# A four-layer macaron kernel on one core: the attention layers put every compute engine in program order, and the last expert's answers leave tile by tile

## The chip, the core and the metric

The kernel runs on one NeuronCore of a Trainium2 chip. The core has TensorE (PE in the profile, with its weight loads as PEld), VectorE (DVE), ScalarE (ACT), GpSimd (POOL) and SyncE (SP, which here only issues DMA transfers). The metric is the device time of one execution, in microseconds.

## The reference

The input x has the shape (4, 512, 128) in float32: four batches of 512 rows. Four layers follow one another, and each is half a feed-forward network, an attention, and half a feed-forward network again, with a layer norm in front of each part and a residual around it:

```
x = x + 0.5 * ffn_l(layernorm(x));  x = x + attn_l(layernorm(x));  x = x + 0.5 * ffn_l(layernorm(x))
```

The parts differ from layer to layer:

- Layer 0: a routed network with 8 experts, the best expert for each row, 320 places per expert, hidden size 512. Its attention has 16 heads of 8, causal, with a table of relative positions added to the scores.
- Layer 1: a gated network with 8 experts (the best two, no limit on places) and a shared one. Its attention scores are a product of two products, `logits = A1 * A2 * SCALE`, with factors of rank 4 and 8 per head, causal.
- Layer 2: a network with 8 experts (the best two), and in place of attention a gated recurrence along the rows.
- Layer 3: a routed network with 8 experts, the best two, 512 places per expert. Its attention has 16 heads of 8 without a mask, and a norm of its own on top of the layer norm.

## The kernel before

x stays in SBUF as `xs[b]`, one tile of 128 x 4 x 128 per batch b: 4 tiles of 128 rows.

**Routed networks** (layers 0 and 3, before and after attention: f00, f01, f30, f31) are the class `Mixture`. `tokens` takes one or two batches: `norms` gives the layer norm (per 128-row tile statistics on DVE at L154 and L155, then `rstd` as a power on POOL at L157, then `off`, then the scaled rows). A transpose, the gate's logits (L310), a softmax (L225 to L232), `route` (L207 to L215) and a rank within the expert (L352 and L353) follow. Then `to` (L373) holds each row's place, and POOL scatters the rows into DRAM with one indirect DMA per 128 rows and choice (`disp_f`, L376). `experts` runs over the 8 experts: it loads the expert's rows (`fetch`), transposes them and works out where each answer goes (`prepare`: `lost`, `back`, L427 to L430), multiplies by the two weight matrices (L445, L461), adds the bias (L465, L469), scales (L472) and scatters the answers to DRAM (`res_f`, L473). `combine` reads the answers back per batch (L484) and adds them to x (L485).

**Attention** is one function for layers 0, 1 and 3. Its work is 16 units, four batches by four groups of four heads. The main loop runs over the units u and in each over four row tiles j. Layers 0 and 1 make scores with a table or mask added (L554, L571, L572, L575, L576) for unit u + 1 while unit u is transposed and copied (`weights`, L587, L594, L596) and multiplied with the values (L607). Layer 3 finds the largest score of each row first (`largest`, L554 and the reductions L629), folds it into q (`lowered`, L635 and L637), makes the scores again by key (`by_key`, L554 and L649), and multiplies with the values (`times_values`, L677). Its `largest` runs `lead = 2*NT + 2` half steps ahead, where a unit has 8. All PSUM tiles come from one ring of 8 banks.

Other work rides in the loop as generators, and a call of `next` moves one of them to its next `yield`, a hop:

- `begin(b)`, by `begun`: norm, transpose, heads and values of the next batch. Layer 1's heads are factors that are copied to SBUF (`fac`, two buffers), written to DRAM in nine transfers per batch (L1086, L1090), and read back per unit by `fetch` (L1106); `project` multiplies them (L1113). In layer 3 `begin` has statistics, `r` as a power on POOL (L1284), `off` (L1285), two scaled copies (L1290, L1295); q and k come from L842, L844 and L846, and per unit `project` makes q and k of a group (L852 on ACT, L1313 on POOL).
- `after(b)`, by `go_on`: `tokens` of f01 or f31 for a batch whose attention has ended.
- `beside`: loads of later weights and zeros for later scatters. For layer 3's feed-forward weights, `moe_weights` puts small POOL copies (L500) ahead of the loads.

The order on each engine comes from two sources. Inside `tc.manual_schedule(engines={mybir.EngineType.PE})` around the loop, PE takes its instructions in the order of the program. The other engines, and all of them outside, are ordered by the tile scheduler from its own cost model, so it can move an instruction ahead of others that the program has first. The hops of the loop are placed so:

```
if j % 2 == 0:
    go_on()
else:
    next(beside, None)
...
if (u % NG, j) in ((0, 1), (1, 1), (1, 3)) and u < n_units - NG:
    begun(u // NG + 1)
if j == 1 and u + 2 < n_units:
    start(u + 2)
if j == 3 and fetch is not None and u + 3 < n_units:
    fetch(*units[u + 3])
```

Of the kernel before, what the change touches and what calls it, by code (L numbers as in the profile page):

```python
# [18 lines left out]
P = 128  # L19
# [23 lines left out]
def kernel(ctx: ExitStack, tc: tile.TileContext, a: dict, out: bass.AP):  # L43
# [102 lines left out]
    def norms(srcs, dsts, tag, scalar=False):  # L146
# [11 lines left out]
        if scalar:  # L158
            off = small.tile([P, g], FP, name=f"off_{tag}", tag=f"bn_off{g}")
            nc.vector.scalar_tensor_tensor(off, mv[:, :, 0], -1.0, rstd, ALU.mult, ALU.mult)  # L160
# [20 lines left out]
    def normed(b, tag, scalar=False):  # L181

        n = work.tile([P, NT, D], FP, name=f"n_{tag}", tag="n", bufs=3)
        norm(xs[b], n, tag, scalar)
        yield
        return n
# [36 lines left out]
    def softmax(pool, lg, g, tag):  # L223
        mx = pool.tile([P, g], FP, name=f"smx_{tag}", tag=f"smx_{tag}")
        nc.vector.tensor_reduce(mx, lg, AX.X, ALU.max)  # L225
        pr = pool.tile([P, g, E], FP, name=f"pr_{tag}", tag=f"pr_{tag}")
        nc.vector.tensor_tensor(pr, lg, bc(mx, [P, g, E]), ALU.subtract)
        nc.scalar.activation(pr, pr, AF.Exp)
        sm = pool.tile([P, g], FP, name=f"sm_{tag}", tag=f"sm_{tag}")
        nc.vector.tensor_reduce(sm, pr, AX.X, ALU.add)  # L230
        nc.vector.reciprocal(sm, sm)
        nc.vector.tensor_tensor(pr, pr, bc(sm, [P, g, E]), ALU.mult)  # L232
        return pr
# [4 lines left out]
    class Mixture:  # L238
# [41 lines left out]
        def tokens(self, bs, wT, scalar=False, pool=None):  # L280
# [8 lines left out]
            for n, b in zip(ns, bs):  # L289
                for c in range(k):  # L290
# [6 lines left out]
                    )  # L297
            yield from norms([xs[b] for b in bs], rows, tag, scalar)
# [22 lines left out]
            pr = softmax(pool, plg[:, : G * E].rearrange("p (g e) -> p g e", e=E), G, f"r{G}")  # L321
# [13 lines left out]
            for i, n in enumerate(ns):  # L335
                for c in range(k):
                    nc.gpsimd.tensor_copy(n[:, :, 1 if c else D + 3], counts[:, c, i * NT : (i + 1) * NT])
# [12 lines left out]
            for c in range(k):  # L350
                out = ps[:, c].rearrange("p g e -> p (g e)")
                nc.tensor.matmul(out, before, masks[:, c].rearrange("p g e -> p (g e)"), start=True, stop=False)  # L352
                nc.tensor.matmul(out, ones, pre[:, c, :G, :].rearrange("p g e -> p (g e)"), start=False, stop=True)  # L353
            kept = tile("kept", [P, k, G, E])
# [3 lines left out]
            if k == 2:  # L358
# [6 lines left out]

            spare = tile("spare", [P, k, G])
            nc.gpsimd.tensor_scalar(
                spare, bc_mid(tok_id[:, i0 : i0 + G], [P, k, G]), float(self.rows), None, ALU.add
            )
# [3 lines left out]
            nc.vector.tensor_tensor(to, slot, keep, ALU.subtract)  # L373
            for c in range(k):
# [9 lines left out]
        def experts(self, w):  # L384
# [3 lines left out]
            with tc.tile_pool(name=f"moe_{self.tag}", bufs=2) as pool:  # L388
# [21 lines left out]
                def prepare(e):  # L410
# [14 lines left out]
                    back = pool.tile([P, per], I32, name=f"back{tag}", tag="back", bufs=3)  # L425
                    lost = pool.tile([P, per], FP, name=f"lost{tag}", tag="lost")
# [9 lines left out]
                for e in range(E):  # L436
# [20 lines left out]
                    y = pool.tile([P, per, D], FP, name=f"y{tag}", tag="y", bufs=3)  # L457
                    for s in range(per):
# [6 lines left out]
                    nc.vector.tensor_tensor(  # L465
                        o[:, :whole, :], po[:, :whole, :], bc_mid(b2[:, e, :], [P, whole, D]), ALU.add
                    )
                    if left:
                        nc.vector.tensor_tensor(o[:left, whole, :], po[:left, whole, :], b2[:left, e, :], ALU.add)  # L469
                    for s in range(per):  # L470
                        m = min(P, cap - s * P)
                        nc.scalar.activation(y[:m, s, :], o[:m, s, :], AF.Copy, scale=d[:m, s, D + 1 : D + 2])  # L472
                        nc.gpsimd.indirect_dma_start(  # L473
                            out=self.back[e * per + s][:, :],
                            out_offset=bass.IndirectOffsetOnAxis(ap=back[:m, s : s + 1], axis=0),
                            in_=y[:m, s, :],
                            in_offset=None,
                        )
# [54 lines left out]
    def attention(pool, tag, begin, project, residual, owT, added, after=None, beside=(), fetch=None):  # L533
# [201 lines left out]
        with tc.manual_schedule(engines={mybir.EngineType.PE}):  # L735
            for _ in range(3):
                begun(0)
# [14 lines left out]
            for u in range(n_units + 1):  # L752
                last = u - 1
                now, nxt = u < n_units, u + 1 < n_units
                for j in range(NT):
# [301 lines left out]
    def l1_attn(first, beside):  # L1057
        with tc.tile_pool(name="attn1", bufs=2) as pool:
# [9 lines left out]
            def begin(b):  # L1068
# [8 lines left out]
                for i, w in enumerate(l1["factors"]):  # L1077
# [7 lines left out]
                    if i == 0:  # L1085
                        nc.sync.dma_start(rows[b][i], f)  # L1086
                        continue
                    for r in range(R1):
                        t = rows[b][i]
# [5 lines left out]
                        )  # L1095
                values(b, nT, l1["wv"], None, f"a1_{b}")
# [169 lines left out]
    def l3_attn(beside, after):  # L1266
        (mixed, bT, wvT, bv), owT, ob, gb = l3["attn"]
        with tc.tile_pool(name="attn3", bufs=2) as pool:
            qk = {}

            def begin(b):
# [12 lines left out]
                nc.gpsimd.tensor_tensor(r, r, mhalf.rearrange("p (k t) -> p k t", k=2), ALU.pow)  # L1284
                nc.vector.scalar_tensor_tensor(  # L1285
# [16 lines left out]
                qk[b] = heads(pool, nT, mixed, bT, tag)  # L1302
                values(b, nT, wvT, bv, tag)
# [136 lines left out]
```

## Time and profile before

| | us |
|---|---|
| median of 3 runs | 1677.62 (1672.47 to 1678.33) |
| the profiled execution, its own time | 1679.45 |
| its span, first to last instruction | 1677.7 |
| PE busy | 1304.1 (78%) |
| DVE busy | 825.1 (49%) |
| ACT busy | 731.5 (44%) |
| POOL busy | 696.3 (42%) |
| mean granted PE clock | 0.872 of full speed |

Stages by the timeline, in us from the start of the span: first tokens and loads 0 to 84, f00's experts 84 to 136, layer 0's attention 137 to 371, f01 to 456, layer 1's first network to 545, its attention 545 to 822, the chain from layer 1's second network to f30's tokens 822 to 1122, f30's experts to 1204, layer 3's attention 1204 to 1541, the last tokens to 1581, f31's experts to 1659, the end at 1677.

How to read it: the profile is one execution. A row of the timeline has the start, the busy time, engine and line, the operation with its tiles and shapes, and in brackets how long the engine was idle before it and what ended that. "PE t_a L587 <- DVE top_a L575" in the view of waits means that PE's next instruction for the tile t_a at line 587 was released by DVE's instruction for top_a. PEclk is the clock that TensorE was granted: at 0.50 a busy PE does half the work. DMA share is the mean busy share of the core's 16 DMA engines.

### The profile page before, as it was taken

To read this page: it belongs to the slowest core of one execution; us is meant where nothing else is said; L and a number is where in the kernel's file an instruction comes from. 1 tells how busy PE (TensorE), PEld (TensorE's weight loads), DVE (VectorE), ACT (ScalarE), POOL (GpSimd) and SP (SyncE) were. 2 spreads that over 40 slices of the span, in tenths; PEclk is the share of its full clock that TensorE was granted. 3 is DMA by queue.
4 is the path that set the end of the run, shared out by engine and by line. 5 is a ranking of instruction groups with operands and counts; after the bars stand their busy time and mean duration, and the time that the engine had idled before them with its cause. 6 is when DMAs were issued, how large, how long until landed. Compare 5 with 4: busy or idle time off the path is not lost. (4 is left out here: it accounts for less than half of the span.)

```text
span 1677.7 us, 27621 instructions
## 1 busy us (share of the span) xinstructions
PE 1304.1 (78%) x9995; PEld 843.8 (50%) x9995; DVE 825.1 (49%) x2817; ACT 731.5 (44%) x1531; POOL 696.3 (42%) x753
## 2 busy tenths in 40 slices
PE   3496999987678699889898667319579999998394
PEld 3274766765555467666567546316333333333262
DVE  3126666652343455556346555234366666664332
ACT  2134877752252466667633222103236555555131
POOL 3347667752425556557343222443540102022243
PEclk9997999996879699899898768659779998999597
DMA  7320140002231655631042222022204000000223
GB/s 216 103 54 29 65 155 10 8 16 73 63 69 34 170 178 146 181 108 52 19 85 102 102 101 101 26 77 71 82 0 152 1 1 14 1 14 13 70 74 97
DMA packets 103087, 123.04 MB, mean 73 GB/s; under 512 B 9404, under 2 KB 74152, under 8 KB 100904
## 3 DMA queue, kind: packets, MB, share of 16 engines
q1 hardware_dynamic: 96296, 108.07, 21.9%
q0 software_dynamic: 6656, 13.22, 2.4%
q8 instruction: 79, 1.29, 0.3%
q14 instruction: 56, 0.46, 0.1%
HBM read 79.27 MB, written 41.98 MB: 72 GB/s over the span
## 5 line engine op out<-in xcount | busy, mean ns | idle before, releaser
L554 PE MATMUL s_a<-k_a,q_a 32*128 32x512 f32 (+3 forms) x1536 | 298.2, 570 | 36.8 <-DMA k_a<-fac_a 14.6
L572 POOL TENSOR_SCALAR sc_a<-sc_a,top_a 128x128 f32<-128x128 f32 (+3 forms) x256 | 274.1, 1085 | 110.6 <-DVE top_a L571 84.0
L576 ACT ACTIVATE sc_a<-sc_a,top_a 128x128 f32<-128x128 f32 (+3 forms) x256 | 142.5, 562 | 124.4 <-DVE top_a L575 123.5
L649 ACT ACTIVATE w_a<-t_a 128x512 f32<-128x512 f32 x256 | 138.2, 595 | 106.3 <-PE t_a L554 103.4
L554 PEld LDWEIGHTS s_a<-k_a,q_a 32*128 32x128 f32 x1536 | 119.1, 196 | 128.2 <-issue 53.7
L473 POOL DMA_INDIRECT res_f<-y_f,back_f x112 | 109.7, 979 | 177.1 <-ACT y_f L472 147.2
L587 PE MATMUL t_a<-ident,sc_a 128*128 128x128 f32 x1280 | 172.0, 281 | 13.9 <-DVE top_a L575 12.8
L554 PE MATMUL t_a<-ql_a,k_a 32*128 32x512 f32 x512 | 174.5, 668 | 4.7 <-DVE low_a__12513 L629 3.6
L587 PEld LDWEIGHTS t_a<-ident,sc_a 128*128 128x128 f32 x1280 | 145.5, 145 | 30.6 <-DVE top_a L575 13.5
L376 POOL DMA_INDIRECT disp_f<-n_f,to_f x96 | 93.9, 978 | 70.8 <-issue 28.2
L461 PE MATMUL o_f<-w_l,h_f 128*128 128x128 f32 (+1 forms) x896 | 113.5, 282 | 7.5 <-ACT h_f L449 7.0
L461 PEld LDWEIGHTS o_f<-w_l,h_f 128*128 128x128 f32 (+1 forms) x896 | 104.7, 186 | 15.1 <-ACT h_f L449 10.3
L445 PE MATMUL h_f<-dT_f,w_l 128*128 128x320 f32 (+1 forms) x256 | 102.2, 544 | 2.8 <-ACT dT_f L423 2.8
L629 DVE TENSOR_REDUCE low_a__12513<-s_a 128x1 f32<-128x512 f32 x128 | 81.3, 682 | 43.1 <-PE t_a L554 36.3
L594 ACT ACTIVATE w_a<-t_a 128x256 f32<-128x256 f32 (+2 forms) x192 | 94.6, 518 | 17.5 <-PE t_a L587 17.0
L607 PE MATMUL acc_a<-w_a,vpad 128*32 128x128 f32 x2560 | 98.5, 281 | 0.0
L629 DVE TENSOR_REDUCE low_a__12515<-s_a 128x1 f32<-128x512 f32 x128 | 80.4, 684 | 34.2 <-PE t_a L554 33.0
L165 ACT ACTIVATE n_f<-x,off_f,rstd_f 128x128 f32<-128x128 f32 x112 | 45.4, 483 | 118.0 <-DVE off_f L160 118.0
L472 ACT ACTIVATE y_f<-o_f,d_f 128x128 f32<-128x128 f32 (+1 forms) x112 | 36.2, 390 | 136.7 <-DVE o_f L465 133.0
L596 ACT COPY w_a<-t_a 128x256 f32<-128x256 f32 (+2 forms) x192 | 92.5, 522 | 0.3 <-PE t_a L587 0.2
L607 PEld LDWEIGHTS acc_a<-w_a,vpad 128*32 128x32 f32 x2560 | 63.5, 110 | 56.9 <-issue 48.9
L575 DVE CUSTOM_DVE_ANT_0 sc_a<-s_a,future 128x128 f32<-128x128 f32 (+3 forms) x128 | 62.4, 487 | 60.0 <-PE s_a L554 54.9
(336 smaller groups left out, 2233.6 us busy)
## 6 DMA issues: line engine op xcount, KB each, us to landing
gb_f<-rows_f SPq DMA_DIRECT2D x16, 1024.0 KB
fac_a<-fac_a_sb SPq DMA_DIRECT2D x36, 256.0 KB
disp_f<-zeros_f SPq DMA_DIRECT2D x4, 2080.0 KB
d_f<-disp_f SPq DMA_DIRECT2D x32, 260.0 KB
w_l<-in_L_ffn_w_dram SPq DMA_DIRECT2D x16, 512.0 KB
cb_f<-rows_f SPq DMA_DIRECT2D x16, 512.0 KB
q_a<-fac_a SPq DMA_DIRECT2D x32, 256.0 KB
k_a<-fac_a SPq DMA_DIRECT2D x32, 256.0 KB
```

The source lines that it names most:

```text
L376: nc.gpsimd.indirect_dma_start(out=self.to[c][i0 + t][:, :], out_offset=bass.IndirectOffsetOnAxis(ap=to[:, c, t : t + 1], axis=0), in_=ns[ ...
L445: nc.tensor.matmul(ps[u][:, :cap], w1[:, e, (c + u) * P : (c + u + 1) * P], dT, start=True, stop=True)
L461: nc.tensor.matmul(po[:m, s, :], h[:, c, s * P : s * P + m], w2[:, e, c, :], start=(c == 0), stop=(c == NC - 1),)
L473: nc.gpsimd.indirect_dma_start(out=self.back[e * per + s][:, :], out_offset=bass.IndirectOffsetOnAxis(ap=back[:m, s : s + 1], axis=0), in_ ...
L554: nc.tensor.matmul(ps[:, n0:n1], q[r : r + SLOT, i * P : (i + 1) * P], k[r : r + SLOT, n0:n1], start=True, stop=True)
L572: nc.gpsimd.tensor_scalar(sc, sc, top, None, ALU.subtract)
L576: nc.scalar.activation(sc, sc, AF.Exp, bias=top, scale=-1.0)
L587: nc.tensor.transpose(ps[:, x * n + j * P : x * n + (j + 1) * P], st["sc", u, i, r0 + x][:, j * P : (j + 1) * P], ident,)
L594: nc.scalar.activation(w[:, : each * n], ps[:, : each * n], AF.Exp)
L607: nc.tensor.matmul(st["acc", u][r * SLOT : (r + 1) * SLOT, i * P : (i + 1) * P], vpads[b % 2][:, j, g * 4 + r, :], st["w", u, i, r][:, j * ...
L629: nc.vector.tensor_reduce(st["low", u][:, i, c : c + 1], ps, AX.X, ALU.max, negate=True)
L649: nc.scalar.activation(w, ps, AF.Exp)
```

## The change

1. The loop's region orders PE, DVE, ACT and POOL by the program. SP isn't named.
2. `begin` has five hops in place of three, at (u % 4, j) = (0,0), (0,1), (0,3), (1,1), (1,3), and `begun(0)` is called five times at the start. Norm and its application are hops apart, heads and values as well; in layer 3 `off` comes a hop after the power. Heads and factors are made at (1,1) where they were made at (1,3).
3. `go_on` is called at every j in place of every second. `tokens` has three more hops: behind the logits, behind the exponential, and behind the rank; one lies ahead of the scatters. The copies of `counts` (POOL) come just ahead of the scatters, and `spare` (POOL) at the very start.
4. `off` in `norms` is made by two POOL instructions in place of one on DVE.
5. `back` has 8 buffers (3), `lost` 4 (2), `y` 4 (3).
6. For the last expert, bias, scale and scatter follow each tile of 128 rows as soon as its matmuls are issued. The other experts still do all whole tiles together.

```diff
@@ norms
-            nc.vector.scalar_tensor_tensor(off, mv[:, :, 0], -1.0, rstd, ALU.mult, ALU.mult)
+            nc.gpsimd.tensor_scalar(off, mv[:, :, 0], -1.0, None, ALU.mult)
+            nc.gpsimd.tensor_tensor(off, off, rstd, ALU.mult)
@@ normed
-        norm(xs[b], n, tag, scalar)
-        yield
+        yield from norms([xs[b]], [n], tag, scalar)
@@ softmax
         nc.scalar.activation(pr, pr, AF.Exp)
+        yield
@@ tokens
+            spare = pool.tile([P, k, G], FP, name=f"spare_{tag}", tag=f"spare{k}{G}")
+            nc.gpsimd.tensor_scalar(
+                spare, bc_mid(tok_id[:, i0 : i0 + G], [P, k, G]), float(self.rows), None, ALU.add
+            )
             yield from norms([xs[b] for b in bs], rows, tag, scalar)
...
-            pr = softmax(pool, plg[:, : G * E].rearrange("p (g e) -> p g e", e=E), G, f"r{G}")
+            yield
+            pr = yield from softmax(pool, plg[:, : G * E].rearrange("p (g e) -> p g e", e=E), G, f"r{G}")
...
-            for i, n in enumerate(ns):
-                for c in range(k):
-                    nc.gpsimd.tensor_copy(n[:, :, 1 if c else D + 3], counts[:, c, i * NT : (i + 1) * NT])
...
                 nc.tensor.matmul(out, ones, pre[:, c, :G, :].rearrange("p g e -> p (g e)"), start=False, stop=True)
+            yield
             kept = tile("kept", [P, k, G, E])
...
             nc.vector.tensor_tensor(to, slot, keep, ALU.subtract)
+            yield
+            for i, n in enumerate(ns):
+                for c in range(k):
+                    nc.gpsimd.tensor_copy(n[:, :, 1 if c else D + 3], counts[:, c, i * NT : (i + 1) * NT])
@@ experts, prepare
-                    back = pool.tile([P, per], I32, name=f"back{tag}", tag="back", bufs=3)
-                    lost = pool.tile([P, per], FP, name=f"lost{tag}", tag="lost")
+                    back = pool.tile([P, per], I32, name=f"back{tag}", tag="back", bufs=8)
+                    lost = pool.tile([P, per], FP, name=f"lost{tag}", tag="lost", bufs=4)
@@ experts
-                    y = pool.tile([P, per, D], FP, name=f"y{tag}", tag="y", bufs=3)
+                    y = pool.tile([P, per, D], FP, name=f"y{tag}", tag="y", bufs=4)
+
+                    def biased(m, t0, t1):
+                        nc.vector.tensor_tensor(
+                            o[:m, t0:t1, :], po[:m, t0:t1, :], bc_mid(b2[:m, e, :], [m, t1 - t0, D]), ALU.add
+                        )
+
+                    def sent(s, m):
+                        nc.scalar.activation(y[:m, s, :], o[:m, s, :], AF.Copy, scale=d[:m, s, D + 1 : D + 2])
+                        nc.gpsimd.indirect_dma_start(
+                            out=self.back[e * per + s][:, :],
+                            out_offset=bass.IndirectOffsetOnAxis(ap=back[:m, s : s + 1], axis=0),
+                            in_=y[:m, s, :],
+                            in_offset=None,
+                        )
+
+                    at_once = 1 if e == E - 1 else whole
                     for s in range(per):
...
+                        if s >= whole or (s + 1) % at_once == 0:
+                            first = s if s >= whole else s + 1 - at_once
+                            biased(m, first, s + 1)
+                            for t in range(first, s + 1):
+                                sent(t, m)
@@ attention
-        with tc.manual_schedule(engines={mybir.EngineType.PE}):
-            for _ in range(3):
+        E_ = mybir.EngineType
+        with tc.manual_schedule(engines={E_.PE, E_.DVE, E_.Activation, E_.Pool}):
+            for _ in range(5):
                 begun(0)
...
-                    if j % 2 == 0:
-                        go_on()
-                    else:
+                    go_on()
+                    if j % 2:
                         next(beside, None)
...
-                    if (u % NG, j) in ((0, 1), (1, 1), (1, 3)) and u < n_units - NG:
+                    if (u % NG, j) in ((0, 0), (0, 1), (0, 3), (1, 1), (1, 3)) and u < n_units - NG:
                         begun(u // NG + 1)
@@ begin of layers 0, 1 and 3
                 qk[b] = heads(pool, nT, mixed, bT, f"a0_{b}")
+                yield
                 values(b, nT, wvT, bv, f"a0_{b}")
...
                 nc.gpsimd.tensor_tensor(r, r, mhalf.rearrange("p (k t) -> p k t", k=2), ALU.pow)
+                yield
                 nc.vector.scalar_tensor_tensor(
```

In layer 1 the same `yield` stands behind the writes of the factors.

More of the change, by code (lines that the diff above doesn't have):

```diff
@@ L364, in tokens @@
             nc.vector.tensor_reduce(keep, kept, AX.X, ALU.add)
[L366 to L369, printed above, removed]
             nc.vector.tensor_tensor(slot, slot, spare, ALU.add)
@@ L464, in experts @@
                             )
[L465 to L478, printed above, removed]
+                        if s >= whole or (s + 1) % at_once == 0:
[3 more added lines that the diff above has]
+                                sent(t, m)
         def combine(self, b):
@@ L1087, in begin @@
                         continue
+                    t = rows[b][i]
                     for r in range(R1):
-                        t = rows[b][i]
                         nc.sync.dma_start(
@@ L1284, in begin @@
                 nc.gpsimd.tensor_tensor(r, r, mhalf.rearrange("p (k t) -> p k t", k=2), ALU.pow)
+                yield
                 nc.vector.scalar_tensor_tensor(
@@ L1302, in begin @@
                 qk[b] = heads(pool, nT, mixed, bT, tag)
+                yield
                 values(b, nT, wvT, bv, tag)
```

## The prediction

> **What bounds the kernel now.** I read the page first. TensorE (PE) is busy 78% of the span, the next engine 49%, so the question in each stage is what PE waits for. A change of 0.5% (8.4 us) is about what a measurement of this kernel can tell from none.
>
> ```profile
> span 1677.7 us, 27621 instructions
> PE 1304.1 (78%) x9995; PEld 843.8 (50%) x9995; DVE 825.1 (49%) x2817; ACT 731.5 (44%) x1531; POOL 696.3 (42%) x753
> ```
>
> Second, PE's waits inside the attention stages, from the view of waits (microseconds in total, times, longest). L1 attention is 545-822, L3 attention 1204-1541:
>
> ```profile
> PE t_a L587 <- DVE top_a L575: 9.4, 4, 3.5
> PE s_a L554 <- DVE fac_a_sb L128: 5.8, 1, 5.8
> ...
> PE s_a L554 <- POOL k_a L1313: 7.9, 1, 7.9
> PE t_a L554 <- DVE low_a__12513 L629: 3.6, 2, 1.8
> PE low_a L635 <- DVE low_a__12513 L629: 2.8, 2, 1.9
> ```
>
> The first two are L1, the rest L3. They are few and short: inside attention PE is nearly always fed. They sit where a batch changes, and the windows view shows that each also costs clock afterwards (columns: length, then busy and count per engine, clock, DMA share, GB/s):
>
> ```profile
> 608.00:616.00 8.00, 4.87 (x54) 3.72 (x53) 2.10 (x10) 2.59 (x7) 1.83 (x2) 0.95 1.02 301
> 616.00:624.00 8.00, 7.98 (x76) 5.41 (x80) 5.88 (x19) 5.26 (x10) 7.14 (x6) 0.63 0.81 244
> ...
> 1372.00:1380.00 8.00, 6.21 (x43) 2.56 (x39) 6.92 (x31) 4.08 (x8) 0.31 (x2) 0.98 0.00 0
> 1380.00:1388.00 8.00, 8.00 (x29) 3.33 (x30) 3.27 (x8) 1.68 (x3) 0.00 (x0) 0.50 0.00 0
> ```
>
> In the last row PE is busy throughout and does half the work: clock 0.50. Third, the timeline at the start of L3 attention:
>
> ```profile
> 1217.05 3.78 PE L842 MATMUL qk_a<-nT_a,wmixed_l 128*128 128x512 f32 x4 [0.87 <-ACT nT_a L1300]
> ...
> 1220.67 1.23 DVE L1285 SCALAR_TENSOR_TENSOR off_a<-mv_a,r_a 128x8 f32<-128x8 f32 x1 [4.18 <-POOL r_a L1284]
> ...
> 1225.39 1.22 DVE L1285 SCALAR_TENSOR_TENSOR off_a<-mv_a,r_a 128x8 f32<-128x8 f32 x1 [2.50 <-POOL r_a L1284]
> 1226.53 0.74 DVE L844 TENSOR_SCALAR q_a<-qk_a,bmixed_l 128x512 f32<-128x512 f32 x1
> ```
>
> Batch 0's q waits for nothing but its turn: two `off` of later batches, hoisted in front of it by the scheduler, hold VectorE (DVE) until 1226.53. Fourth, the end of an expert stage (f01):
>
> ```profile
> 447.72 0.42 DVE L465 TENSOR_TENSOR o_f<-o_f,b_l 128x256 f32<-128x256 f32 x1 [2.56 <-PE o_f L461]
> 448.06 0.27 DVE L469 TENSOR_TENSOR o_f<-o_f,b_l 64x128 f32<-64x128 f32 x1
> 448.18 0.98 ACT L472 ACTIVATE y_f<-o_f,d_f 128x128 f32<-128x128 f32 x3 [3.58 <-DVE o_f L465]
> 448.86 0.96 POOL L473 DMA_INDIRECT res_f<-y_f,back_f  x1 [1.97 <-ACT y_f L472]
> 450.12 0.96 POOL L473 DMA_INDIRECT res_f<-y_f,back_f  x1 [0.31 <-issue]
> ```
>
> The scatters are 1.26 us apart and nothing else runs: the tail is on the path.
>
> [...] after a gap of 3.60 us at 1338.72 the 512-wide matmul of L554 takes 1.06 to 1.22 us, before it 0.59 to 0.69. [...] DMA share 1.02 at 301 GB/s in 608-616, where factors and q/k loads overlap.
>
> **The change part by part**, against the profiled execution's own 1679.45 us (span 1677.7 and 1.75 around it; the median of the runs is 1677.62, 1.8 lower).
>
> *Last expert by tiles.* Before, the bias (0.42 + 0.27), the first scale and all scatters follow the last matmul. f01: last scatter issued 451.39; if tiles 0 and 1 leave while PE still computes, only the third (64 rows) remains: about 0.3 + 0.4 + one scatter, 1.9 us sooner. Cap 512 (f30, f31): four scatters 1.26 apart of which three go ahead, less what POOL still owes the expert before (f31: till 1651.55): about 3. Price: two or three more short DVE ops, beside PE. Four tails: 2 × 1.9 + 2 × 3 ≈ **−9** (−6 to −11).
>
> *Buffers.* `back` may not be rewritten while its scatter is in flight: DVE waits for res_f 41.4 us in 20 waits. In f00/f01 an expert takes 6.02 us with PE busy throughout, so nothing is won there. In f31 experts take 8.77, 7.97 and 8.25 us against an undisturbed 7.44 in f30; some of that is the loads of d_f. **−4** (0 to −9).
>
> *L3's start.* In program order k and q follow qk at about 1221, k_a (0.76 each on POOL, L1313) at 1222, first scores 1222.6 instead of 1230.45: **−8**. Bounds −10 to +6: combine's adds of later batches (to about 1216) may stand ahead.
>
> *L3's batch starts.* The stats of the next batch and of the finished batch's tokens fall together on DVE (1331-1336), then `off` waits 1.75 for POOL. Loss by clock and gaps in 1332-1348: 3.6 idle + 0.35 × 8 of clock, about 7; two later ones about 3 each, 13 in all. With stats at (0,0), `off` a hop later and tokens from (1,1), the two lie a unit apart and `off` finds its power done: **−10** (0 to −13).
>
> *L3's routing.* Loss 1372-1396: 1.79 idle + 0.50 × 8 + 0.34 × 8 ≈ 8.5; 1452-1476 about 7. The yields split off two ops and the rank, but some 21 DVE ops of 0.22 us pitch, 4.6 us, stay in one hop; in order they stand ahead of the L629 reductions. And tokens now take 8 j instead of 10, so the third batch's routing, 1531-1536 in the drain before, moves into the loop. **+4** (−6 to +10). The drain itself stays: batch 3's stats end 1551.04, POOL's older scatters at 1551.12, so their removal wins nothing.
>
> *L1's boundaries.* Moving a step moves all of it: three factor matmuls, three copies, nine DMA writes of 256 KB on SP's queue, then values and POOL's row add. Before, factors at (1,3) are written 738.96 to 744.7, and the q/k loads that they release end too late: DVE's q product waits 5.34, POOL's k product 5.99, PE 3.53 and then clock 0.59 for 8 us: about 7. The first boundary (616.02) loses 7 alike, the second 11, where the 4 MB of layer 3's weights collide (DVE copy waits 7.62 for a write, PE 5.83). Half a unit earlier is about 7 us, more than the 6 waited: −25 at best. What is late next is the third factor copy (two buffers: it waits for the first write), now in DVE's order with the scores behind it; and the weights, held by POOL copies in order until u = 8, j = 3, can collide with the third boundary. SP's order stays the scheduler's. **−17** (+3 to −25).
>
> *Smaller.* L1's norm stall (722-730, PE 1.60) and L0's waits (PE t_a L587 for DVE, 3.4 in three): **−5** (0 to −8). `off` becomes two POOL ops: nearest row L156 on POOL, 0.24 us, against 0.17 on DVE; about 0.3 more per norm, some seven on a path: **+2** (0 to +4). The moved copies and `spare` (0.2 to 0.3 each on POOL) hide under scatters and PE.
>
> *The price of a fixed order.* The trace cannot show it. Nine places (three batch changes in three layers) get a hop of norm, heads, routing or scatter in DVE, ACT and POOL queues. A scatter hop is 4 × 1.26 in L0 and 8 × 1.26 = 10 us on POOL in L3; behind it stand k_a, the power, and in L0 the subtractions L572. L0's scores run a unit ahead, L3's only two half steps over a unit (`lead`). Each place costs 0 to 8.5 (the loss of 1372-1396); L1's start and the tokens outside attention stay. I take one of nine in full: **+8** (0 to +35; below nothing only through orders that I cannot see, −10).
>
> Sum: −9 −4 −8 −10 +4 −17 −5 +2 +8 = **−39**. 1679.45 − 39 = 1640.5, against the median 1638.6; I say **1638**.
>
> **Rivals.**
> A (0.57): as above, 1605 to 1660.
> B (0.18): L1's boundaries stay, limited by the DMA engines rather than by when factors are made: −39 + 17 = −22, **1656**. For it: DMA share 1.02 and 1.00 there. Against: the queue is at 0.11 in 580-600, so there is room earlier.
> C (0.13): the scheduler's order was near the program's already, and only tails and buffers count: −13, **1665**. Against: the order at 1220-1226 isn't the program's.
> D (0.12): slower. DVE blocks in order behind a chunk or a late transfer, PSUM banks fill, PE idles and its clock halves, 8.5 us a place. Without the price the sum is −47, so it decides from six of nine places on; all nine give +76 − 47 = +29, **1707**. For it: 1372-1388 shows exactly this with 4.6 us of DVE work, and lead in L3 is short. Against: scores run ahead a unit in L0 and L1.
>
> **Numbers.** Faster by over 0.5% (below 1669): all of A, nearly all of B, most of C: 0.82. Within 0.5%: a third of C and a little of B and D: 0.08. Slower: 0.10. Range 1604 to 1678: A to C with the bounds of L1 and the start; D's upper part and luck in every term are left out.
>
> **What would show it.** Right: first scores under 7 us after qk in L3; no PE wait over 3 us at L1's second and third boundary; POOL's last two res_f scatters of a stage not back to back behind one ACT row; DVE back_f waits for res_f gone. Wrong: PE waits for DVE L629 or L575 over 2 us in more than six places, clock at 0.5 in slices where it is 1.00 now, or POOL idle before disp_f in a loop while L572 is late.

## The result and the profile after

The changed kernel takes 1656.96 us (1652.67 to 1660.23), the kernel before 1676.32 beside it: ratio 0.9888, interval 0.9861 to 0.9915. That is 19.4 us less, where 39 were forecast: the right way, and half the size. The profiled execution has a span of 1656.6 us against 1677.7.

The first lines of the page:

```profile
span 1656.6 us, 27617 instructions
PE 1301.9 (79%) x9995; PEld 836.5 (50%) x9995; DVE 834.5 (50%) x2803; ACT 740.4 (45%) x1531; POOL 708.1 (43%) x797
```

PE's work is the same, 9995 matmuls; 21 us of the span are gone. PE's waits in the two attention stages, L1 (555 to 825) first, then L3 (1205 to 1540); columns as before, total, times, longest:

```profile
PE s_a L567 <- POOL k_a L1128: 13.4, 1, 13.4
PE s_a L567 <- ACT w_a L607: 5.9, 3, 4.1
PE s_a L567 <- ACT fac_a_sb L130: 4.1, 2, 3.2
...
PE s_a L567 <- POOL k_a L1330: 12.4, 4, 5.9
PE s_a L567 <- DVE otok_a L713: 3.8, 2, 1.9
```

The first line is the wait for L1's first keys, which the kernel before has as well:

```profile
PE s_a L554 <- DMA k_a<-fac_a: 14.6, 1, 14.6
```

The waits of before inside the loops (DVE top_a 9.4, fac_a_sb 5.8, DVE low_a) are gone or small. New ones stand in their place, on ACT and on POOL: these two engines now do something else first. Layer 1's first boundary (the first change of batch in its loop) in the windows view:

```profile
602.00:610.00 8.00, 7.88 (x108) 6.14 (x106) 6.03 (x26) 5.31 (x12) 5.53 (x5) 1.00 0.97 301
610.00:618.00 8.00, 8.00 (x95) 6.33 (x88) 4.43 (x21) 5.99 (x14) 6.75 (x8) 1.00 0.88 243
```

Where PE was busy 4.87 of 8 us and then ran at clock 0.63, it is now fed throughout at full clock, with the DMA engines nearly as full as before (share 0.97 and 0.88, against 1.02 and 0.81). The start of layer 3:

```profile
1209.90 2.93 PE L855 MATMUL qk_a<-nT_a,wmixed_l 128*128 128x512 f32 x3 [0.87 <-ACT nT_a L1316]
...
1212.01 0.75 DVE L857 TENSOR_SCALAR q_a<-qk_a,bmixed_l 128x512 f32<-128x512 f32 x1 [3.99 <-PE qk_a L855]
...
1215.33 3.19 PE L567 MATMUL s_a<-k_a,q_a 32*128 32x512 f32 x19 [0.19 <-POOL k_a L1330]
```

q comes as soon as its matmul has ended, and the first scores 5.4 us after q and k began, where it was 13.4. The end of f01's experts:

```profile
453.60 0.29 DVE L465 TENSOR_TENSOR o_f<-o_f,b_l 128x128 f32<-128x128 f32 x1 [0.65 <-PE o_f L483]
453.92 0.40 ACT L470 ACTIVATE y_f<-o_f,d_f 128x128 f32<-128x128 f32 x1 [1.54 <-DVE o_f L465]
453.94 1.16 PE L483 MATMUL o_f<-w_l,h_f 128*128 128x128 f32 x8 [0.45 <-DVE o_f L465]
454.60 0.96 POOL L471 DMA_INDIRECT res_f<-y_f,back_f  x1 [0.95 <-ACT y_f L470]
...
457.60 0.90 POOL L471 DMA_INDIRECT res_f<-y_f,back_f  x1 [0.51 <-ACT y_f L470]
```

Bias, scale and scatter of one tile run beside the matmuls of the next, and only the last tile's are left over.

Stage by stage, from the timelines: the lengths are differences of start times (q and k's first matmul, last projection, first scores, first and last transpose of an expert's rows, first load of answers; where the timeline merges equal instructions into a row, the row's start). The four last columns are the first experiments, told below: e1 has only PE in order, e2 leaves ACT free, e3 POOL, and e4 is the kernel before with the order alone.

| stage, us | before | after | e1 | e2 | e3 | e4 |
|---|---|---|---|---|---|---|
| four expert stages, transposes | 193.6 | 183.6 | 183.2 | 182.9 | 182.8 | 193.2 |
| four tails, to the load of answers | 69.9 | 60.9 | 60.9 | 60.9 | 60.9 | 70.2 |
| L0 attention | 231.2 | 239.0 | 233.5 | 231.9 | 239.2 | 251.1 |
| f01's answers to L1's first scores | 108.8 | 102.2 | 105.0 | 102.4 | 102.9 | 103.1 |
| L1 attention from there | 258.0 | 256.2 | 261.9 | 249.1 | 271.2 | 279.1 |
| L3, q and k to first scores | 13.4 | 5.4 | 13.4 | 5.4 | 5.4 | 5.4 |
| L3 attention from there | 317.5 | 319.7 | 311.6 | 338.8 | 305.2 | 334.9 |

Tails and buffers alone are 19.0 of the 21.1 us. Attention wins 8.0 + 6.6 + 1.8 and loses 7.8 + 2.2 in its stages. That would be 25.4; the other 4.3 us are lost outside these stages, in the first tokens, behind the ends of L0 and L3, and the rest.

### The profile page after: what moved, and what is told of

Its sections match the earlier page's. It is cut to its first block, busy times and chain, and to the rows that moved or that the text cites. A ratio compares the mean times of both kernels' runs of the same rounds, so it can differ in the third digit from the quotient of the medians.

```text
span 1656.6 us, 27617 instructions
## 1 busy us (share of the span) xinstructions
PE 1301.9 (79%) x9995; PEld 836.5 (50%) x9995; DVE 834.5 (50%) x2803; ACT 740.4 (45%) x1531; POOL 708.1 (43%) x797
## 5 line engine op out<-in xcount | busy, mean ns | idle before, releaser
L567 PE MATMUL s_a<-k_a,q_a 32*128 32x512 f32 (+3 forms) x1536 | 314.9, 551 | 50.5 <-POOL k_a L1128 13.4
L567 PEld LDWEIGHTS s_a<-k_a,q_a 32*128 32x128 f32 x1536 | 122.5, 191 | 157.2 <-issue 48.7
L567 PE MATMUL t_a<-ql_a,k_a 32*128 32x512 f32 x512 | 170.1, 666 | 0.5 <-DVE ql_a L650 0.5
L450 PE MATMUL h_f<-dT_f,w_l 128*128 128x320 f32 (+1 forms) x256 | 105.0, 547 | 2.7 <-ACT dT_f L428 2.7
L588 DVE CUSTOM_DVE_ANT_0 sc_a<-s_a,table 128x128 f32<-128x128 f32 (+3 forms) x128 | 62.5, 488 | 58.9 <-PE s_a L567 45.7
L620 PEld LDWEIGHTS acc_a<-w_a,vpad 128*32 128x32 f32 x2560 | 63.2, 110 | 55.5 <-issue 45.8
```

The costliest lines, as they stand in the source:

```text
L450: nc.tensor.matmul(ps[u][:, :cap], w1[:, e, (c + u) * P : (c + u + 1) * P], dT, start=True, stop=True)
L567: nc.tensor.matmul(ps[:, n0:n1], q[r : r + SLOT, i * P : (i + 1) * P], k[r : r + SLOT, n0:n1], start=True, stop=True)
L588: nc.vector.tensor_tensor_reduce(sc, banks[r][:, :n], more, -1.0, HUGE, ALU.add, ALU.min, top)
L620: nc.tensor.matmul(st["acc", u][r * SLOT : (r + 1) * SLOT, i * P : (i + 1) * P], vpads[b % 2][:, j, g * 4 + r, :], st["w", u, i, r][:, j * ...
```

## The experiments

The theory after the result: the buffers, tails and starts do what they should or more, and in the loops a fixed order gives back what the finer hops win, because an instruction that waits holds everything behind it on its engine, as eight scatters on POOL hold k_a, and with it PE for 5.88 us. The rival: the order makes no difference and the hops' places alone moved the times. A unit's time, below, is the time from one unit's transposes of its result (`ot_a`) to the next unit's; an undisturbed unit is one that no batch change or scatter touches.

**e1: only PE in order.**

```
-        with tc.manual_schedule(engines={E_.PE, E_.DVE, E_.Activation, E_.Pool}):
+        with tc.manual_schedule(engines={E_.PE}):
```

> The changed kernel with its hops, buffers and tiles, but only TensorE in program order; DVE, ACT and POOL are the scheduler's again. Theory 1 (a fixed order brings blocking at the head of a queue: in layer 0 every unit takes 13.18 us instead of 12.00, in layer 3 eight scatters hold k_a for 5.9 us): layer 0's undisturbed unit is back at 12.0 and its stage about 7 us shorter, the two k_a waits are gone (14 us with the clock they cost), but the start of layer 3 loses its 8 us and the batch starts some 4: about 1648, 1640 to 1658. Theory 2 (the order is nearly the scheduler's own; the finer hops made all the difference): 1655 to 1659, units as in the changed kernel.

Measured 1657.28, ratio 0.9882 (0.9859 to 0.9905): the time of the changed kernel. Read by the sum, theory 2 holds. The table shows why the sum misleads: L0's undisturbed unit is back at 12.00 us, as in the kernel before and against 13.18 in the changed one, L0 wins 5.5 and L3's loop 8.1, while L3's start loses its 8.0, L1's way in 2.8 and L1 5.7. On top of the new hops the fixed order is a gain and a loss of about one size.

**e2: ACT left to the scheduler.** `engines={E_.PE, E_.DVE, E_.Pool}`.

> The changed kernel with PE, DVE and POOL in program order and ACT left to the scheduler. Theory 1: what lengthens layer 0's unit is ACT's order (the copy q_a ahead of the weights w_a), and in layer 1 ACT waits 3.1 us for off_a at the start and 2.4 to 2.6 for the factor copies: layer 0's unit 12.0 to 12.3, layer 1's first batch about 7 us shorter, in all 1640 to 1646. Rival: it is POOL or DVE that sets layer 0's unit, and ACT only shows it: the unit stays at 13.18 and the time at 1655 to 1660.

Measured 1662.91, 0.9913 (0.9891 to 0.9935): neither number. The reading by stages is clear, though. L0's unit is 12.00 and its stage 7.1 us shorter, L1 7.1 shorter, and L3's loop 19.1 longer, where PE now waits 4.5 us for ACT (k_a, w_a in front of ot_a) besides POOL; the rest of the 19 was not traced. So ACT's order costs 7 us each in L0 and L1, and 19 us are lost in L3 without it. The first timeline is the changed kernel, at the end of a unit in L0, the second this run:

```profile
196.71 0.51 ACT L589 ACTIVATE sc_a<-sc_a,top_a 128x256 f32<-128x256 f32 x1 [0.18 <-DVE top_a L588]
...
197.06 0.93 PE L567 MATMUL s_a<-k_a,q_a 32*128 32x384 f32 x6
197.12 0.71 ACT L865 ACTIVATE q_a<-q_a,own 128x512 f32<-128x512 f32 x1
...
197.74 0.85 ACT L607 ACTIVATE w_a<-t_a 128x384 f32<-128x384 f32 x2
...
198.26 0.91 PE L567 MATMUL s_a<-k_a,q_a 32*128 32x384 f32 x2 [0.28 <-ACT w_a L607]
```

```profile
191.86 0.51 ACT L589 ACTIVATE sc_a<-sc_a,top_a 128x256 f32<-128x256 f32 x1 [0.59 <-DVE top_a L588]
...
192.28 0.47 ACT L607 ACTIVATE w_a<-t_a 128x384 f32<-128x384 f32 x1
...
192.65 0.50 ACT L589 ACTIVATE sc_a<-sc_a,top_a 128x256 f32<-128x256 f32 x1
...
192.90 0.93 PE L567 MATMUL s_a<-k_a,q_a 32*128 32x384 f32 x8
```

In order, ACT does both exponentials and q_a before the first copy w_a, and PE stops after six of its eight matmuls: the rest wait for that copy, whose PSUM bank they need. The scheduler puts a w_a between. From the first of the eight to PE's next work it takes 2.03 us (197.06 to 199.09) against 0.85 (192.90 to 193.75): 1.18 us, the whole difference of the unit.

**e3: POOL left to the scheduler.** `engines={E_.PE, E_.DVE, E_.Activation}`.

> The changed kernel with PE, DVE and ACT in program order and POOL left to the scheduler. Theory 1: the two k_a waits behind the scatters in layer 3 are gone, about 7 us each, and the unit behind the scatter is 18 to 19 us instead of 25.4 and 23.7; layer 0's unit stays at 13.18: 1643 to 1649. Rival: the scheduler puts the scatters ahead of k_a as well, since they are ready earlier: 1655 to 1659.

Measured 1657.65, 0.9884 (0.986 to 0.9909): the rival's number, but the theory's stages. L3's loop is 14.5 us shorter, the units behind the scatters 17.17 and 15.78 instead of 25.44 and 23.70, and L0's unit stays at 13.18. The sum hides it, because L1 loses 15.0. Part of that is that ACT, in order, waits for what POOL now does late (for off_a 10.0 us where it was 3.8, and PE for ACT's w_a 12.1 where it was 5.9); part is one factor copy that waits 7.1 us for a write, 2.6 before, and why was not traced. The place of L3 in the changed kernel:

```profile
1362.27 1.10 POOL L381 DMA_INDIRECT disp_f<-n_f,to_f  x1 [13.19 <-DVE low_a__12536 L642]
1363.67 0.96 POOL L381 DMA_INDIRECT disp_f<-n_f,to_f  x1 [0.30 <-ACT w_a L662]
...
1371.26 0.96 POOL L381 DMA_INDIRECT disp_f<-n_f,to_f  x1 [0.30 <-issue]
1372.26 0.77 POOL L1330 TENSOR_SCALAR k_a<-k_a,own,next_row 128x512 f32<-128x512 f32 x1
1373.08 1.22 PE L567 MATMUL s_a<-k_a,q_a 32*128 32x512 f32 x1 [5.88 <-POOL k_a L1330]
```

Eight scatters, 1.26 us apart, then k_a, then PE, after 5.88 us without work and at half clock (1.22 us for the matmul, which took 0.69 at 1365.47; clock 0.50 from 1373 to 1375). With POOL free the same unit's k_a goes ahead of them:

```profile
1362.94 0.77 POOL L1330 TENSOR_SCALAR k_a<-k_a,own,next_row 128x512 f32<-128x512 f32 x1 [2.44 <-PE t_a L567]
...
1372.37 1.10 POOL L381 DMA_INDIRECT disp_f<-n_f,to_f  x1 [0.74 <-DVE low_a__12536 L642]
```

**e4: the order alone**, in the kernel before, nothing else.

> The kernel before with nothing changed but the four engines' order in attention. Theory 1: blocking costs at least as much as in the changed kernel, since the hops are coarser (heads and values in one, softmax, route and rank in one or two), while the start of layer 3 wins its 8 us: 1680 to 1700, with layer 0's unit at 13.2. Theory 2: within 5 us of 1676.

Measured 1723.69, 1.0271 (1.0249 to 1.0293): 46 us slower, more than theory 1 said. L0 loses 19.9, L1 21.1, L3's loop 17.4, and the two starts win 8.0 and 5.7. Its waits are longer than those of the kernel before, and many are rival D's, for DVE (L1's first, then L3's):

```profile
PE t_a L587 <- DVE top_a L575: 10.3, 5, 3.8
PE s_a L554 <- ACT w_a L594: 9.0, 2, 4.5
PE s_a L554 <- DVE top_a L575: 6.6, 2, 6.4
...
PE t_a L554 <- DVE low_a__12515 L629: 5.9, 3, 2.0
PE t_a L554 <- DVE low_a__12513 L629: 5.1, 2, 2.5
```

In L0 the undisturbed unit is 13.18 us, as in the changed kernel. So the theory that the order makes no difference is out, and the finer hops are what makes it bearable.

**e5 and e5b: tiles and buffers alone**, in the kernel before (parts 5 and 6 of the change). The second run has the changed kernel beside it on one chip.

> The kernel before with only the last expert's tiles and the larger rings of back, lost and y; attention is as before. If the stage table of the two traces is read rightly, the four tails give about 9 us and the buffers 9 to 10 (6 in f31, 2.6 in f30, the rest in f00): 1659, 1656 to 1662, so nearly the whole gain of the change, and attention's part is near nothing. Rival: part of the shorter expert stages comes from what attention leaves to POOL and DMA, and this gives 10 to 14 us only: 1664 to 1668.

> The kernel with only tiles and buffers again, now beside the changed kernel on one chip. In the trace of the first run f31's experts took 51.7 us from first to last transpose (57.9 before, 51.8 after the change), so if the account by stages holds, this one lies 14 to 19 us under the kernel before: ratio 0.989 to 0.992. Rival: 8 to 13 us, 0.992 to 0.995, and the rest of the changed kernel's gain is made in attention.

> The changed kernel itself, as a yardstick on the same chip. By the account, attention's gains (start of layer 3, 8 us; batch starts of layer 3, some 13; boundaries of layer 1, 11; start of layer 1, 6) and its new losses (layer 0's unit 7 to 8, layer 1's start and third boundary 9, layer 3's scatters 14) nearly cancel: 0.986 to 0.990, 1 to 7 us under the kernel with tiles and buffers alone. Rival: if attention's part is a clear gain, 10 us or more under it.

Measured 0.9937 (0.9903 to 0.997), then 0.9918 (0.9896 to 0.994): 1683.03 against 1696.04, 13.0 us. The changed kernel beside it: 1670.30, 0.984 (0.9815 to 0.9865). Expected were 14 to 19 us for the parts alone, and that attention adds 1 to 7: on this chip attention adds 12.7, so both runs gave what their rivals said, and the account was wrong in its balance. The expert stages are as in the changed kernel (183.3 us in the first of these runs). These runs, and all below, were on other chips than the first pair and e1 to e4; there the kernel before takes 1695 to 1702 us. On them PE, DVE and ACT pause for 1 to 3.6 us at a time with no cause recorded, mostly around scatters, and such pauses fall into the tails of f30 and f31, which are 19 us instead of 17.

Where the 12.7 come from can be read all the same, for e5b has the attention of the kernel before and was traced beside the changed kernel. L0 loses 4.2 us there instead of 7.8, and L3's loop, which lost 2.2 on the first chip, wins 7.2; the starts and L1 win as before (8.0, 5.1 and 3.3). It is the old order that is slower on this chip, at its scatters: its two units with scatters in L3 take 22.77 and 20.09 us where the kernel before on the first chip took 18.26 and 16.94, those in L0 14.17 and 14.23 instead of 11.98. The changed kernel's are 25.06 and 23.59 in L3, as on the first chip, and 14.46 and 14.57 in L0. So the scatter hops lose 13.9 us against the old order on the first chip and 5.8 on this one. Below, units that hold no scatter are compared across chips, which agree (13.18, 12.00, 15.77), and times only with the changed kernel on the same chip, or, where it did not run there, with its ratios 0.984 and 0.9817 (e7's pair) on the two other chips.

**e6: scatters in four hops**, in the changed kernel.

```
                         in_offset=None,
                     )
+                    if k == 2 and len(bs) == 1 and t % 2 == 1:
+                        yield
```

> The changed kernel, with the eight scatters of layer 3's tokens in four hops of two. Theory: k_a passes between them, no PE wait for it over 1 us, units behind a scatter 17 to 19 instead of 25.4 and 23.7: 1642 to 1648. Rival: k_a waits as long in pieces, because the queue still holds 10 us of scatters within two j of need, or the third batch's scatters slip into the drain: 1652 to 1658.

Measured 1660.85, 0.9805 (0.9774 to 0.9837). The changed kernel did not run on this chip; against its 0.984 and 0.9817 on two others the gain is 0.1 to 0.4%, 2 to 6 us, and the intervals overlap. The total therefore doesn't show it. The trace does. PE's longest waits in L3's loop:

```profile
PE s_a L569 <- DVE otok_a L715: 3.7, 2, 1.9
PE low_a L650 <- DVE low_a__12536 L644: 1.9, 1, 1.9
```

The wait for k_a is gone, and the units behind the scatters take 19.19 and 17.75. To end this wait, splitting a hop is enough; POOL need not be freed.

**e10: q and k started at j = 0** in layers 0 and 3.

```
-                    if j == 1 and u + 2 < n_units:
+                    if j == (0 if fetch is None else 1) and u + 2 < n_units:
```

> The changed kernel with the next unit's q and k started at j = 0 instead of j = 1 in layers 0 and 3 (layer 1 as it is). Theory: in layer 0 the copy q_a (0.71 us) no longer stands between the scores' exponentials and the copies w_a that free the PSUM banks, and the unit falls from 13.18 to about 12.4, 5 to 8 us in the stage; in layer 3 k_a comes before the scatters and its waits go, 14 us: 1637 to 1646. Rival: it is the wait for DVE's scores, not q_a, that holds w_a back, and the unit stays at 13.2: only layer 3 wins, 1643 to 1650.

Measured 0.9785 (0.9753 to 0.9817). L0's unit is 12.57, half of the way from 13.18 to 12.00: q_a's place is one half of ACT's cost there, something else in ACT's order the rest (e2); the order of exponentials and copies is the likely one, not shown. In L3 the k_a wait is gone, but the units behind the scatters still take 23.32 and 21.79. PE waits for DVE's ql_a there (4.3 us in three), behind the last scatter, where DVE, ACT and PE stand still together. What the split does beyond letting k_a through is left open; e9, below, has the same.

**e8: the scaled rows a j later.**

```
-  if (u % NG, j) in ((0, 0), (0, 1), (0, 3), (1, 1), (1, 3)) and u < n_units - NG:
+  if (u % NG, j) in ((0, 0), (0, 2), (0, 3), (1, 1), (1, 3)) and u < n_units - NG:
```

The reason is this piece of the changed kernel, at L1's start:

```profile
568.91 6.89 POOL L585 TENSOR_SCALAR sc_a<-sc_a,top_a 128x384 f32<-128x384 f32 x6
...
577.64 0.20 POOL L161 TENSOR_TENSOR off_a<-off_a,rstd_a 128x4 f32<-128x4 f32 x1
...
577.87 1.65 ACT L166 ACTIVATE n_a<-x,off_a,rstd_a 128x128 f32<-128x128 f32 x4 [3.10 <-POOL off_a L161]
579.42 0.84 ACT L607 ACTIVATE w_a<-t_a 128x384 f32<-128x384 f32 x2
...
579.95 1.64 PE L567 MATMUL s_a<-k_a,q_a 32*128 32x384 f32 x2 [4.13 <-ACT w_a L607]
```

The statistics were done at 572.6, 3 us before the norm's first step on POOL began, but its POOL steps queue behind the subtractions, the scaled rows behind them on ACT, the copies w_a behind those, and PE behind all.

> The changed kernel, with the second hop of begin (the scaled rows) at (0,2) instead of (0,1). Theory: the norm queues on POOL behind a unit's subtractions, and ACT, which has the scaled rows next in its order, waits for it with the copies w_a behind; a j later the norm is done, so layer 1's first unit ends 6 to 7 us earlier after its first scores (33 us instead of 39.7) and each batch start of layer 1 wins 1 to 4 more: 8 to 12 us less than the changed kernel. Rival: the wait only moves on to T_a at (0,3), and the time is within 3 us of the changed kernel.

Measured 0.976 (0.9732 to 0.9788), 1657.57 against 1670.30 of the changed kernel on the same chip: 12.7 us less, a little more than expected. From first scores to the end of L1's first unit it takes 33.9 us instead of 39.5, and two boundary units fall from 15.33 to 13.55. In its trace w_a goes ahead, and the scaled rows wait only 0.35:

```profile
579.19 0.87 ACT L607 ACTIVATE w_a<-t_a 128x384 f32<-128x384 f32 x2
...
582.92 1.65 ACT L166 ACTIVATE n_a<-x,off_a,rstd_a 128x128 f32<-128x128 f32 x4 [0.35 <-POOL off_a L161]
```

**e7: three factor buffers**, `tag="fac", bufs=3`, with the changed kernel beside it.

> The changed kernel with three buffers for layer 1's factors instead of two, so that the third copy doesn't wait for the first write. Theory: ACT's waits of 1.4, 2.6 and 2.4 us for the write are gone, the units at the boundaries fall from 15.3 to 13.6 and the third from 24.7 by 3: 5 to 8 us under the changed kernel. Rival: eight rows of the network's norm stand in front of the factor copies anyway and the writes, not the copies, are late: 0 to 3 us.

> The changed kernel again, as the yardstick of this call: 0.984 to 0.989 of the kernel before.

Measured 0.9777 (0.9746 to 0.9808) against 0.9817 (0.9786 to 0.9847), 1664.34 against 1670.28: 5.9 us, though the intervals overlap. PE's wait for fac_a_sb L130 (3.4 us) is gone and the third boundary's unit is 20.55 instead of 24.83; the other boundary units stay at 15.33, against the theory. The missing buffer is the third boundary's trouble only.

**e9, e12, e13: combinations.** e9 has `E_.PE, E_.DVE` and `E_.Pool if added else E_.Activation`. e12 has all four in L3, ACT free in L0 and L1, split scatters, late rows and three factor buffers. e13 is e12 with all four in L1 too.

> The changed kernel with PE, DVE and POOL in program order in layers 0 and 1, and PE, DVE and ACT in layer 3. If the layers don't act on one another, the stages of the two runs with one engine left out add up: layer 0 and 1 end 18 us before the kernel before as with ACT free, layer 3 takes 310.6 from its q and k to the last projection as with POOL free, in all 1627 to 1633. Rival: the gain of ACT free in layer 1 comes from the placement of transfers in that one schedule: 1636 to 1645.

> The version that the runs point to: PE, DVE and POOL in program order in layers 0 and 1, all four in layer 3; scatters of layer 3 in four hops; scaled rows at (0,2); three buffers for the factors. Adding up: layer 0 7 us and layer 1 7 us under the changed kernel as with ACT free, layer 3's scatters 14, layer 1's start 6: about 30 us under the changed kernel, ratio 0.970 to 0.975. Rival: the gains overlap (ACT free already takes the wait of the factor copies, a free ACT moves the late rows forward again): 0.976 to 0.982.

> As the version before it (ACT free in layer 0, all four in order in layer 3, split scatters, late rows, three factor buffers), but with all four in order in layer 1. Theory: with the two places mended, a fixed ACT order costs nothing in layer 1, since its q and k are made by DVE and POOL and no copy q_a stands in ACT's order; with the first unit at 33.9 us instead of 37.5 it is 3 to 6 us shorter: 0.958 to 0.961 of the kernel before. Rival: the third boundary keeps its 24.6 us in ACT's order (21.3 with ACT free), which takes it back: 0.961 to 0.964.

Measured: e9 1652.09, 0.9754 (0.9723 to 0.9784); e12 0.962 (0.9589 to 0.965), 1630.94 against 1670.30 of the changed kernel; e13 0.9569 (0.9532 to 0.9605), 1628.17 against 1670.28. e12 and e13 are better than expected and beat both kernels; e13 is 4.3% under the kernel before.

e9 is a miss: against the changed kernel's ratios it is 0.6 to 0.9% faster, 11 to 15 us, where the sum of the stages promised 24 to 30. That is nearer the rival, but not for the rival's reason, since L1 stays within 1 us of e2's. L3 has POOL free as in e3, and k_a comes ahead of the scatters here too, but the units behind them take 24.33 and 21.88 us instead of 17.17 and 15.78. In place of the wait for k_a stands a pause behind the last scatter, with DVE idle for 2.30 us and ACT for 1.69 until 1363.1, and then PE at half clock by the time of its matmul (1.19 us, against 0.59 to 0.69 at clock 1.00 in the first pair of traces):

```profile
1360.46 0.96 POOL L381 DMA_INDIRECT disp_f<-n_f,to_f  x1 [0.30 <-issue]
1363.95 1.19 PE L567 MATMUL t_a<-ql_a,k_a 32*128 32x512 f32 x1 [1.97 <-DVE ql_a L650]
```

So what e3 won in L3 is shown on its chip only; on this one the pause costs about as much as the wait for k_a did. Of the runs on the later chips only those with the split have short units there (e6, e12, e13: 17.6 to 20.75 us).

PE's waits in L1 (560 to 830) of e13, below one pause of 5.4 us with no cause recorded, which lies behind the loop and is in the traces of all runs:

```profile
...
PE s_a L569 <- ACT w_a L609: 1.8, 3, 0.8
PE s_a L569 <- ACT fac_a_sb L1098: 1.3, 1, 1.3
```

L1's loop takes 237.6 us there, 247.1 in e12, and ACT's order in L1 is all that differs: with the two places mended it is a gain in L1. The totals, from two chips, differ by 2.8 us only.

## Why the prediction was half right

**Tails, forecast −9: right.** 69.9 to 60.9, and each tail by nearly the steps of the sum: 1.7, 1.8, 2.8, 2.7, where 1.9 and 3 were said. These steps add up to 9.8, not 9.

**Buffers, −4: mis-sized.** The four expert stages lose 10.0: 6.1 in f31, 2.6 in f30, 1.3 in the others. The list of f31's experts (8.77, 7.97, 8.25) was short: from one expert's transposes to the next's the kernel before has 11.37, 7.68, 8.03 and 8.77 us there, and in f30, from which the undisturbed 7.44 was taken, also 8.69 and 9.29. After the change all of these are 7.45, so little was left over for the loads of d_f. DVE's back_f no longer waits for res_f at all; the three larger rings were not tried one by one.

**L3's start, −8: right** to the tenth: 13.4 to 5.4.

**L3's batch starts, −10: right, a little small.** The units (b,0) and (b,1) of the three later batches sum to 119.4 before and 105.8 after: 13.6, the whole loss that was counted.

**L3's routing, +4: it costs nothing in sum.** The routing units take 63.2 before and 62.6 after. The third batch's does cost in the loop (15.81 to 18.40), the others win as much.

**L1's boundaries, −17: the first two right, the third not.** From the first unit's end the loop wins 9.0: 5.9 and 5.4 in the first two batches, and it loses 2.3 in the last two. What was said to be late next, the third copy and layer 3's weights, is what may hold the third boundary; e7 shows the copy's part, 4.3 us in that unit, and no run takes the weights away. I named both and still counted most of the gain.

**L1's start, held for unchanged: wrong both ways.** The way from f01's answers to the first scores is 6.6 shorter. The order alone does 5.7 of that (e4), the hops alone 3.8 (e1); the two don't add up. Then the first unit takes 7.2 longer (e8).

**L0, −3 of waits: wrong sign, +7.8.** The waits for DVE that were forecast to go did go, 3.1 us of waits for ACT's w_a came in eleven places, and each undisturbed unit became 1.18 us longer. The +2 for `off` on POOL was not measured alone; e8 shows that its queue costs more than its work (ACT waits 3.10 us for an off_a whose last step takes 0.20).

**The step that failed is the price of a fixed order.** The prediction counted nine places at a batch change and took one at 8.5 us, +8. The runs show three things in its place: L0's unit, in every unit and not at a batch change (7.1 us in the stage, e2); L1's start, 5.6 to 7.2 us (e8); the two scatter hops of L3, 25.44 − 18.26 and 23.70 − 16.94, 13.9 us (e3, e6). Together about 27, inside the bound of 35 and far from the value taken; without it the sum was −47, and −21 − 27 = −48 is what the first pair of traces gives. That this closes so well is in part luck, since buffers and batch starts won 10 us more than forecast and L1's boundaries 8 less. On e5b's chip, where the old order loses at its scatters as well, the third part is 5.8 us and not 13.9. The scatter hop and its 10 us ahead of k_a stand in the prediction word for word; it had not asked how long k_a can wait, which is two j, about 8 us by the undisturbed unit of 15.77. ACT's order in L0 was not in it at all: it counted the chunks that a batch change adds, not the program's everyday order against the scheduler's.

**Rival B gave 1656, the measured time, by coincidence:** its reason is not what happened, for the first two L1 boundaries opened with the DMA engines nearly as full as before. **Rival C**, tails and buffers only, describes one pair of traces well (19.0 of 21.1) but not the mechanism, and on another chip attention adds 12.7 us to it. **Rival D**'s blocking is there, mostly on ACT and POOL and not on DVE, short of the point where it decides, and past it in e4.

**Its signs.** Of those for right, the first scores came (5.4 us), the waits of back_f are gone and the tails overlap; L1's third boundary kept a wait of 3.2 us. Of those for wrong, a lower clock where it was full came in L3 (0.71 from 1374 to 1382, behind the wait for k_a; as far into the same unit the kernel before has 1.00, from 1394.9 to 1402.9). None of them named the causes, k_a behind scatters on POOL and w_a behind q_a on ACT.

**A reading to correct.** The prediction says that each of PE's waits also costs clock afterwards. Not each does: in the kernel before, the one of 1.60 us at 727.37 is followed by clock 1.00 from 727 to 743. The one of 1.79 us at 1379.86, PE's only idle time from 1372 to 1388, is followed by 0.50 and 0.66 in two slices of 8 us, in which PE is busy throughout, and the one of 3.60 us at 1338.72 by 0.65 from 1340 to 1348. Why the two short ones differ stays open.

In both of the places that no sign named, the later instruction came only after those in front of it: k_a at 1372.26 on POOL, behind eight scatters that began at 1362.27, and w_a at 197.74 on ACT, behind q_a at 197.12. The price lay in who stands first.

## What to carry to other kernels

To put an engine in program order makes the program's order a schedule, so price it engine by engine and layer by layer: for each instruction that can wait, or that comes in a burst, ask what stands behind it and how long that can be late. Two stages that are chained by a queue want a distance, here the statistics and their use more than one step apart (e8: L1's first unit ends 33.9 us after its first scores instead of 39.5); a burst of scatters is better split, so that short work passes (e6: the units behind the scatters take 19.19 and 17.75 us, against 25.44 and 23.70 in the changed kernel on the first chip). A total that does not move when an order is taken away (e1) may hide a gain and a loss of some 15 us each: read stages before believing it. And a gain in a stage on one chip (e3) is worth a second look on another (e9).

## What the hardware showed unasked

On the chips of the later runs PE, DVE and ACT pause with no cause in the records more often: 10 to 17 idle times of over 0.9 us in each trace, against 4 or 5 in those of the first pair and of e1 to e4. Four long ones of 2.6 to 5.4 us, in layer 1's networks, stand in all traces; the ones that come in addition are 0.9 to 3.6 us, mostly around scatters. POOL's scatters have the same pitch, 1.26 us, in the changed kernel's traces on the first and a later chip and in e13's. A unit with scatters in L0 takes 14.2 to 14.4 us there with tiles and buffers alone, against 11.98 in the kernel before on the first chip, where attention is the same code. The cause stays open.
